# Columns picked by hand in a graph kernel: register loads moved to a fixed place in each unit, and an earlier request for the destination indices

## The chip, the cores and the metric

The kernel runs on one core of one Trainium2 chip. The metric is device time in microseconds of one execution. Nine executions of the kernel before were timed: median 5463.57 us, from 5436.52 to 5480.25 us.

## The reference: what is computed

One layer of a graph network over 12,500 nodes of 128 features and 400,000 edges, which come sorted by destination `dst`. With `h = relu(layernorm(x))`:

```
m   = relu(concat(h[src], h[dst], ea) @ w1 + b1) @ w2 + b2      # per edge; ea has 32 features
agg = segment_sum(m, dst)                                       # per node
gi  = agg @ w_ih + b_ih ;  gh = h @ w_hh + b_hh                 # a GRU cell
r, z = sigmoid(i_r + h_r), sigmoid(i_z + h_z) ;  n = tanh(i_n + r * h_n)
out = x + (1 - z) * n + z * h
```

Everything is float32.

## The kernel before, in words

**Stages.** A first stage (about the first 350 us) normalises the nodes, keeps `h` transposed in on-chip memory (`hT_all`, 128 features by 12,500 nodes) and writes the table `A = h @ w1[0:128]` to device memory. After it the edges are walked in 391 *pairs* (the change's words call them double groups) of 8 tiles of 128 edges; a pair is two *units* `u = 2k` and `u = 2k + 1` of 4 tiles each. Python loops write the instructions of all 782 units out one after another; each engine has one list of instructions in that order and runs it in order. No scheduler moves anything.

**One pair `k`.** POOL fetches the 1,024 rows `A[src]` with 8 indirect DMAs (line 146) into a buffer `G`; seven such buffers go round, and the next pair's fetch starts when the relu of the second unit of an older pair has let its buffer go. `Ld` holds the destinations of the edges, copied to 64 partitions; DVE compares them with node numbers to a one-hot matrix in the upper half of `L` (`onehot_T`, line 495); the lower half of `L` holds the edge features, which SP loads directly (line 485). `window` copies 2 x 32 columns of `hT_all` (`hw`, line 514), PE multiplies them by `w1[128:256]` (`oh`, line 517), and `window_rows` adds the bias into `RW` in two DVE instructions (line 526). PE then multiplies `L` by `RW` (`pre`, line 592), DVE adds the fetched rows (`add`, line 617), ACT applies the relu into `RB` (line 623), and PE sums the edges per node with a second one-hot matrix `OH` (DVE line 544; PE line 636, `seg`). `take` copies the sums out (DVE line 644, ACT line 645). Every 14 pairs a block of 512 nodes goes through the GRU in small steps (`node`).

**Pairs by hand.** 43 of the 391 pairs are not fetched by POOL. For 19 of them ACT, and for 18 DVE, collects the 1,024 columns `hT_all[:, src]` one instruction a column (lines 788 and 790); PE then multiplies them by `w1[0:128]` (line 603), and DVE's add of line 617 falls away. For the other 6 SP fetches the rows with one small DMA each (line 795). The address of a column is a register. An instruction of the engine itself, TENSOR_LOAD (line 782), loads 32 of these registers at a time, so a job of 1,024 columns has 32 such loads. A job is spread evenly over the units between the last pair of its kind and its own (36 to 46 units): `run_jobs` is called four times in a unit (phases 0 to 3), each time does as many groups of 4 columns as are due, and a load falls wherever 32 columns have been used up.

**Order within unit `u`:** phase 0 of the jobs; `take` (even units); `stages`: `onehot_T` (even) or `onehot` (odd) three pairs ahead, `pre(u + 3)`, `add(u + 2)`, `relu(u + 2)`; phase 1 of the jobs and `window` (even); phase 2; `seg(u)`; phase 3, `window_rows` (even) and a step of `node`.

**SP's list.** At every fourth unit `fetch(q + 2)` asks for `L` (256 KB) and then for `Ld` (two DMAs of 128 KB) of two pairs; both tiles have three buffers. Between them stand the row fetches of SP's own jobs.

Of the kernel before, what the change touches and what calls it, by code (L numbers as in the profile page):

```python
# [8 lines left out]
F32 = mybir.dt.float32  # L9
# [12 lines left out]
GRP = 4  # L22
# [5 lines left out]
V = 32  # L28
# [14 lines left out]
PLACE = 20  # L43
CH = PLACE * PAIR
LOAD = 32
STEP = {"act": 4, "dve": 4, "sp": 2}
SPREAD = {"act": 19, "dve": 18, "sp": 6}
NR = 12672

H_AT = 16512  # L50
# [6 lines left out]
def tile_gnn(ctx: ExitStack, tc: tile.TileContext, x, src, srcT, dstT, dstP, eaT, eaP, w1, b1, w2T, b2,  # L57
# [26 lines left out]

    mode, order = {}, {m: [] for m in SPREAD}
    for m, n in SPREAD.items():
        lo = JOBS0 + 15
        for i in range(n):
            k = lo + int((i + 0.5) * (NP - 2 - lo) / n)
            while k in mode:  # L90
                k += 1
            mode[k] = m
            order[m].append(k)
# [385 lines left out]
    def fetch(q):  # L479
        if q * QP >= NP:  # L480
            return
        n = min(QP, NP - q * QP)
        Ls[q] = p3.tile([128, QP * 512], F32, name="L")
        c = slice(q * QP * 512, (q * QP + n) * 512)
        nc.sync.dma_start(Ls[q][2 * V:, :n * 512], eaP[:, c])
        Ds[q] = p3.tile([2 * V, QP * 512], I32, name="Ld")
        for a in range(2):
            nc.sync.dma_start(Ds[q][V * a:V * (a + 1), :n * 512],
                              dstP[a:a + 1, c].to_broadcast([V, n * 512]))

    def onehot_T(k):
        if k >= NP:
            return
        c = slice((k % QP) * 512, (k % QP + 1) * 512)
        nc.vector.tensor_scalar(Ls[k // QP][:2 * V, c], Ds[k // QP][:, c], node_of[:, k:k + 1],  # L495
                                None, op0=ALU.is_equal)


    bases, PB_ = {}, {}

    def window(k):
        if k >= NP:
            return
        b = k // BP
        if k % BP == 0:
            n = min(BP, NP - k)
            _, vals = nc.values_load_multi_w_load_instructions(
                base_i[0:1, b, 0:n], engines=[ET.DVE], min_val=0, max_val=LAST,
                skip_runtime_bounds_check_because="clamped above")
            for i, v in enumerate(vals):  # L510
                bases[k + i] = v
        hw = p3.tile([128, 2, V], F32, name="hw", bufs=2)
        s = hT_all[:, bass.ds(bases.pop(k), V + SHIFT)]
        nc.vector.tensor_copy(hw, bass.AP(tensor=s.tensor, offset=s.offset,  # L514
                                          ap=[list(s.ap[0]), [SHIFT, 2], [1, V]]))
        PB_[k] = ps2.tile([128, 512], F32, name="oh")
        nc.tensor.matmul(PB_[k][:2 * V, :D], hw.rearrange("p a v -> p (a v)"), w1b,  # L517
                         start=True, stop=True)

    def window_rows(k):  # L520
        if k >= NP:
            return
        pm = PB_.pop(k)
        for a in range(2):
            s = slice(V * a, V * (a + 1))
            nc.vector.tensor_tensor(RW[k % 4][s, a, :], pm[s, :D], b1b[s, :], op=ALU.add)  # L526
# [80 lines left out]
    def add(u):  # L607
        if u >= NU:
            return
        if u in HE or u // 2 in hand:  # L610
            RT[u] = PP.pop(u)
            HE.pop(u, None)
            if u % 2:
                hand.pop(u // 2, None)
        else:
            RT[u] = unit(u)
            nc.vector.tensor_tensor(RT[u], PP.pop(u), RT[u], op=ALU.add)  # L617

    def relu(u):
        if u >= NU:  # L620
            return
        o = RB[u % 3]
        nc.scalar.activation(o[:, :, :D], RT.pop(u), AF.Relu)  # L623
        if u % 2:
            G.pop(u // 2, None)
# [142 lines left out]
        nc.sync.dma_start(at[r:r + 1, :], src[t0 * 128:(t0 + PAIR) * 128].rearrange(  # L768
            "(o e) -> o e", o=1))

    def one_by_one(m, k):
        et = {"act": ET.Activation, "dve": ET.DVE, "sp": ET.SP}[m]
        r = by_hand.index(k)
        if m == "sp":
            G[k] = pj[0].tile([128, GRP, 2, D], F32, name="G_sp", bufs=1)
            rows = G[k].bitcast(U8)
        else:
            hand[k] = pj[0].tile([128, PAIR * 128], F32, name=f"HE_{m}")
            he = hand[k].bitcast(U8)
        for e0 in range(0, PAIR * 128, LOAD):  # L780
            low, high = (0, ROW * (N - 1)) if m == "sp" else (H_AT, H_AT + 4 * (N - 1))
            _, vals = nc.values_load_multi_w_load_instructions(
                at[r:r + 1, e0:e0 + LOAD], engines=[et], min_val=low, max_val=high,
                skip_runtime_bounds_check_because="src holds numbers of nodes")
            for i, v in enumerate(vals):
                e = e0 + i
                if m == "act":
                    nc.scalar.copy(he[:, e * 4:e * 4 + 4], h_bytes[:, bass.ds(v - H_AT, 4)])  # L788
                elif m == "dve":
                    nc.vector.tensor_reduce(he[:, e * 4:e * 4 + 4],  # L790
                                            h_bytes[:, bass.ds(v - H_AT, 4), None],
                                            AX.X, ALU.max)
                else:
                    a, j = divmod(e // 128, GRP)
                    nc.sync.dma_start(rows[e % 128:e % 128 + 1, j, a, :],
                                      A_bytes[bass.ds(v, ROW)].rearrange("(o f) -> o f", o=1))
                if i % STEP[m] == STEP[m] - 1:
                    yield


    jobs = {}
    for m, kl in order.items():
        start = 2 * JOBS0
        for k in kl:
            end = 2 * k - (8 if m == "sp" else 4)
            jobs.setdefault(start, []).append((m, k, end - start))
            start = end if m != "sp" else 2 * k + 2
    live = {}

    PH = 4  # L810

    def run_jobs(u, phase):
        if u == 2 * JOBS0 and phase == 0:
            early.close()
            pj.append(late.enter_context(tc.tile_pool(name="pj", bufs=2, side="right")))
        if phase == 0:
            for m, k, span in jobs.get(u, ()):
                live[m] = [one_by_one(m, k), u, span, PAIR * 128 // STEP[m], 0]
        for m, job in list(live.items()):
            it, start, span, steps, done = job  # L820
            want = -(-steps * ((u - start) * PH + phase + 1) // (span * PH))
            while job[4] < want:
                job[4] += 1
                if next(it, "end") == "end":
                    del live[m]
                    break


    asked = [RAW]
# [9 lines left out]

    gathers(0)  # L840
    for q in range(2):
        fetch(q)
    for k in range(3):
        window(k)
        window_rows(k)


    def stages(u):
        if u + 7 >= 0:
            raw_stats(u + 7)  # L850
        if u + 6 >= 0:
            raw_fin(u + 6)
            raw_h(u + 6)
        if u % 2 == 0:
            onehot_T(u // 2 + 3)
        elif u > -7:
            onehot(u // 2 + 3)
        if u + 4 >= 0:
            raw_turn(u + 4)
        if u + 3 >= 0:  # L860
            pre(u + 3)
        if u + 2 >= 0:
            add(u + 2)
            relu(u + 2)

    for u in range(-7, 0):
        stages(u)
# [12 lines left out]
    for u in range(NU):  # L880
        k, h = divmod(u, 2)
        gathers(u)
        if h == 0:
            if k % QP == 0:
                fetch(k // QP + 2)
            if k % BP == 0 and k:
                nodes_left.append([node(k // BP - 1), 0])
            if k % PLACE == 1:
                indices(k // PLACE + 2)
            if k % PLACE == 5:  # L890
                place(k // PLACE + 1)
                dst_tile(k // PLACE + 2)
            if k == NP - 20:
                check_windows()
        for r in range(2 * u, min(2 * u + 2, NJ)):
            job_indices(r)
        if u == 2 * JOBS0 - 2:
            nc.vector.tensor_scalar(at, at, place_of[:, 0:1], place_of[:, 1:2],
                                    op0=ALU.mult, op1=ALU.add)

        def other(phase):
            run_jobs(u, phase)
            if h == 0 and phase == 1:
                window(k + 3)
            if h == 0 and phase == 3:
                window_rows(k + 3)
            if phase == 3:
                step(nodes_left)

        other(0)  # L910
        if h == 0:
            take(k - 1)
        stages(u)
        other(1)
        other(2)
        seg(u)
        if u == 0:
            node_setup()
        other(3)
# [173 lines left out]
```

## Time and profile before

| | |
|---|---|
| profiled execution, its own time | 5460.47 us |
| its span in the profile | 5458.6 us |
| median of nine executions | 5463.57 us |
| busy: PE, DVE, ACT, POOL | 3100.5, 2706.0, 2737.3, 2658.9 us |
| granted TensorE clock, mean | 0.657 |
| DMA traffic | 325.92 MB, 60 GB/s |

No engine is busy for more than 57% of the span. The forty slices look alike from about 350 us to the end, so one pair in the middle stands for the rest. In the groups of the profile the first number behind the bar is busy time, then the mean of one instruction, then the idle time of that engine in front of the group's instructions and what ended it; "issue" means that the profile shows nothing that the engine waited for. Instructions of an engine's sequencer, such as TENSOR_LOAD, are not counted as busy.

### The profile page before, as it was taken

How to read it: one execution, taken by the hardware profiler on the slowest of the kernel's cores; microseconds unless marked ns; L12 is line 12 of the kernel's file. 1: busy time of each engine (PE TensorE's matmuls, PEld its weight loads, DVE VectorE, ACT ScalarE, POOL GpSimd, SP SyncE). 2: the span in 40 equal slices, each digit the busy share in tenths (PEclk: the TensorE clock that was granted, in tenths of full speed). 3: DMA queues.
4: the chain of work that ended last, by engine and by line, in shares of the span. 5: the costliest groups of instructions: out<-in, count | busy, mean ns of one | idle time of the engine just before them, and what ended most of it. 6: DMA issues, size and time to landing. Idle time of an engine off the chain costs nothing. (4 is left out here: it accounts for less than half of the span.)

```text
span 5458.6 us, 94893 instructions
## 1 busy us (share of the span) xinstructions
PE 3100.5 (57%) x13578; PEld 1856.0 (34%) x13578; DVE 2706.0 (50%) x22515; ACT 2737.3 (50%) x20936; POOL 2658.9 (49%) x2789
## 2 busy tenths in 40 slices
PE   2663454555665656566555556555564656465657
PEld 2442232333333333333333333333332333233434
DVE  3644344545544544555555445554554554544553
ACT  2434344555555555555555555555555555555651
POOL 5345434354545454545554554455454454545562
PEclk7776666666665666566666666666665666666667
DMA  3322111222222122222222222222222221222221
GB/s 110 83 59 56 50 47 52 60 57 61 61 56 60 55 62 56 58 60 58 60 58 59 58 61 58 57 62 60 58 59 60 60 62 55 62 55 60 62 65 37
DMA packets 157887, 325.92 MB, mean 60 GB/s; under 512 B 65058, under 2 KB 77133, under 8 KB 157256
## 3 DMA queue, kind: packets, MB, share of 16 engines
q0 software_dynamic: 88992, 182.43, 12.0%
q1 hardware_dynamic: 68119, 137.33, 9.1%
q14 instruction: 520, 4.25, 0.3%
q8 instruction: 112, 1.84, 0.1%
q10 hardware_dynamic: 144, 0.07, 0.0%
HBM read 305.74 MB, written 13.84 MB: 59 GB/s over the span
## 5 line engine op out<-in xcount | busy, mean ns | idle before, releaser
L146 POOL DMA_INDIRECT G<-A,src_i x2704 | 2585.0, 956 | 2718.7 <-ACT RB L623 1823.5
L788 ACT COPY HE_act<-hT_all 128x4 uint8 x19456 | 2173.5, 191 | 1757.1 <-issue 1740.3
L790 DVE TENSOR_REDUCE HE_dve<-hT_all 128x4 uint8 x18432 | 1404.3, 144 | 1133.4 <-issue 1123.3
L592 PE MATMUL pre<-RW,L 128*128 128x256 f32 x3128 | 1355.7, 572 | 849.8 <-DVE G L617 703.9
L592 PEld LDWEIGHTS pre<-RW,L 128*128 128x128 f32 x3128 | 791.4, 280 | 1223.3 <-issue 707.7
L517 PE MATMUL oh<-w1b,hw 128*64 128x128 f32 x782 | 245.0, 411 | 1342.6 <-DVE hw L514 683.6
L636 PE MATMUL seg<-RB,OH 128*32 128x129 f32 x6250 | 719.6, 372 | 2.5 <-issue 2.5
L623 ACT ACTIVATE RB<-G 128x512 f32<-128x512 f32 x676 | 426.2, 630 | 469.8 <-issue 212.4
L517 PEld LDWEIGHTS oh<-w1b,hw 128*64 128x64 f32 x782 | 103.5, 188 | 1548.5 <-DVE hw L514 778.8
L526 DVE TENSOR_TENSOR RW<-oh,b1b 32x128 f32<-32x128 f32 x782 | 218.1, 279 | 770.0 <-issue 641.4
L617 DVE TENSOR_TENSOR G<-pre,G 128x512 f32<-128x512 f32 x676 | 460.5, 681 | 262.8 <-issue 243.8
L636 PEld LDWEIGHTS seg<-RB,OH 128*32 128x32 f32 x6250 | 384.4, 142 | 281.7 <-issue 183.0
L495 DVE TENSOR_SCALAR L<-Ld,node_of 64x512 f32<-64x512 int32 x391 | 189.6, 485 | 138.5 <-DMA Ld<-in_dstP 90.2
L644 DVE COPY sums<-seg 64x128 f32<-64x128 f32 x391 | 106.5, 272 | 187.2 <-remote 106.3
L645 ACT CAST dcol<-seg 64x1 f16<-64x1 f32 x391 | 60.0, 153 | 225.1 <-DVE sums L644 159.9
L544 DVE TENSOR_TENSOR OH<-dloc,iota 128x256 f32<-128x256 f16 (+1 forms) x392 | 162.1, 414 | 13.6 <-issue 10.8
L667 PEld LDWEIGHTS nd<-spot,sums 64*128 64x128 f32 x782 | 164.1, 320 | 13.3 <-issue 13.3
L667 PE MATMUL nd<-spot,sums 64*128 64x40 f32 x782 | 168.2, 404 | 0.0
L631 PE MATMUL seg<-zrow 1*64 1x129 bf16 x391 | 115.0, 294 | 0.0
L326 PE MATMUL pre<-w1a,hT_all 128*128 128x128 f32 x196 | 51.5, 412 | 77.2 <-issue 57.6
L686 PE MATMUL nd<-DEG,brow 33*128 33x512 f32 x112 | 94.0, 932 | 1.0 <-DVE DEG L654 1.0
L690 PE MATMUL nd<-TOT,w2ih 128*128 128x512 f32 x112 | 89.1, 890 | 0.0
(151 smaller groups left out, 1629.3 us busy)
## 6 DMA issues: line engine op xcount, KB each, us to landing
G_sp<-A SPq DMA_DIRECT2D x6144, 0.5 KB
L<-in_eaP SPq DMA_DIRECT2D x195, 256.0 KB
Ld<-in_dstP SPq DMA_DIRECT2D x390, 128.0 KB
G<-A,src_i POOLq DMA_INDIRECT x2704
xb<-in_x SPq DMA_DIRECT2D x28, 256.0 KB
out<-xb SPq DMA_DIRECT2D x28, 256.0 KB
xs<-in_x SPq DMA_DIRECT2D x11, 512.0 KB
A<-asb SPq DMA_DIRECT2D x11, 512.0 KB
```

Of the source, the lines that this page charges most:

```text
L146: nc.gpsimd.indirect_dma_start(out=G[k][:, j, a, :], out_offset=None, in_=table, in_offset=bass.IndirectOffsetOnAxis(ap=src_i[c][:, i:i + ...
L495: nc.vector.tensor_scalar(Ls[k // QP][:2 * V, c], Ds[k // QP][:, c], node_of[:, k:k + 1], None, op0=ALU.is_equal)
L517: nc.tensor.matmul(PB_[k][:2 * V, :D], hw.rearrange("p a v -> p (a v)"), w1b, start=True, stop=True)
L526: nc.vector.tensor_tensor(RW[k % 4][s, a, :], pm[s, :D], b1b[s, :], op=ALU.add)
L544: nc.vector.tensor_tensor(o, d.to_broadcast(shape), i.to_broadcast(shape), op=ALU.is_equal)
L592: nc.tensor.matmul(PP[u][:, 2 * i:2 * i + 2, :], Ls[k // QP][:, c0:c0 + 128], RW[k % 4], start=True, stop=not raw)
L617: nc.vector.tensor_tensor(RT[u], PP.pop(u), RT[u], op=ALU.add)
L623: nc.scalar.activation(o[:, :, :D], RT.pop(u), AF.Relu)
L636: nc.tensor.matmul(SEG[k][V * a:V * (a + 1), :D + 1], OH[k][:, j, a, :], RB[u % 3][:, (j % 2) * 2 + a, :D + 1], start=False, stop=all(b != ...
L667: nc.tensor.matmul(pt[:, bass.ds(offs[i], V + SHIFT)], sums[:, i, :], spot, start=False, stop=i == n - 1)
L788: nc.scalar.copy(he[:, e * 4:e * 4 + 4], h_bytes[:, bass.ds(v - H_AT, 4)])
L790: nc.vector.tensor_reduce(he[:, e * 4:e * 4 + 4], h_bytes[:, bass.ds(v - H_AT, 4), None], AX.X, ALU.max)
```

## The change

Four things are changed together.

1. **Destinations earlier.** `fetch` is split. `fetch_d` asks for `Ld`, and it is called for `q + 3`, ahead of `fetch(q + 2)`, which asks for `L` alone.
2. **First jobs.** Other pairs are chosen for the hand work (the same numbers: 18, 19 and 6), so that the first job of each kind is about as long as the others. DVE's jobs have 39 or 40 units, ACT's 36 to 40.
3. **Loads once a unit.** While DVE or ACT has a job, it loads 32 registers once in every unit. The load stands right behind a fixed place: DVE's add of line 617 (ACT: the relu of line 623) and the last 7 columns of the load before. The other 25 columns are spread over the four phases: 7 in phase 1, 6 in each of phases 2, 3 and 0. A job is therefore done in 32 units, and in the 4 to 8 units that are left before the next job starts the engine has no columns. SP's job keeps the even spread.
4. **Window.** `hw` is copied before the add of the even unit instead of in phase 1; its matmul stays in phase 1 (`window_b`).

```
-SPREAD = {"act": 19, "dve": 18, "sp": 6}
+TAIL = 7
+SPREAD = {"dve": 18, "act": 19, "sp": 6}
...
-        lo = JOBS0 + 15
+        lo, hi = {"dve": (JOBS0 + 3, NP - 14), "act": (JOBS0 + 11, NP - 6),
+                  "sp": (JOBS0 + 5, NP - 10)}[m]
         for i in range(n):
-            k = lo + int((i + 0.5) * (NP - 2 - lo) / n)
+            k = lo + int((i + 1) * (hi - lo) / n)
...
+    def fetch_d(q):
...
+        HW[k] = hw
+
+    def window_b(k):
...
+    class Job:
...
+        def run(self, left=0):
+            while len(self.vals) > left:
...
+    def behind(m, u):
+        if m in live:
+            live[m].run()
+            if live[m].e == PAIR * 128:
+                del live[m]
+        begin(m, u + 1)
+        if m in live:
+            j = live[m]
+            if j.loaded < PAIR * 128:
+                j.load(LOAD)
+            assert j.span * LOAD >= PAIR * 128
+
+    PARTS = (1, 2, 3, 0)
+
     def run_jobs(u, phase):
...
+        for m in ("act", "dve"):
+            if m in live:
+                n = max(0, len(live[m].vals) - TAIL)
+                live[m].run(TAIL + n - -(-n // (4 - PARTS.index(phase))))
...
         if u % 2 == 0:
             onehot_T(u // 2 + 3)
+            if u >= 0:
+                window(u // 2 + 3)
...
             add(u + 2)
+            behind("dve", u)
             relu(u + 2)
+            behind("act", u)
...
             if k % QP == 0:
+                fetch_d(k // QP + 3)
                 fetch(k // QP + 2)
...
             if h == 0 and phase == 1:
-                window(k + 3)
+                window_b(k + 3)
```

More of the change, by code (lines that the diff above doesn't have):

```diff
@@ L45 @@
 LOAD = 32
-STEP = {"act": 4, "dve": 4, "sp": 2}
-SPREAD = {"act": 19, "dve": 18, "sp": 6}
+TAIL = 7
+SPREAD = {"dve": 18, "act": 19, "sp": 6}
 NR = 12672
@@ L482, in fetch @@
         n = min(QP, NP - q * QP)
+        c = slice(q * QP * 512, (q * QP + n) * 512)
         Ls[q] = p3.tile([128, QP * 512], F32, name="L")
+        nc.sync.dma_start(Ls[q][2 * V:, :n * 512], eaP[:, c])
+    def fetch_d(q):
+        if q * QP >= NP:
+            return
+        n = min(QP, NP - q * QP)
         c = slice(q * QP * 512, (q * QP + n) * 512)
-        nc.sync.dma_start(Ls[q][2 * V:, :n * 512], eaP[:, c])
         Ds[q] = p3.tile([2 * V, QP * 512], I32, name="Ld")
@@ L496, in onehot_T @@
                                 None, op0=ALU.is_equal)
-    bases, PB_ = {}, {}
+    bases, PB_, HW = {}, {}, {}
     def window(k):
@@ L515, in window @@
                                           ap=[list(s.ap[0]), [SHIFT, 2], [1, V]]))
+        HW[k] = hw
+    def window_b(k):
+        if k >= NP:
+            return
         PB_[k] = ps2.tile([128, 512], F32, name="oh")
-        nc.tensor.matmul(PB_[k][:2 * V, :D], hw.rearrange("p a v -> p (a v)"), w1b,
+        nc.tensor.matmul(PB_[k][:2 * V, :D], HW.pop(k).rearrange("p a v -> p (a v)"), w1b,
                          start=True, stop=True)
@@ L769, in job_indices, with __init__, load @@
             "(o e) -> o e", o=1))
[L771 to L780, printed above, removed]
+    class Job:
+        def __init__(self, m, k, start, span):
+            self.m, self.k, self.start, self.span = m, k, start, span
+            self.e, self.loaded, self.vals = 0, 0, []
+            self.r = by_hand.index(k)
+            if m == "sp":
+                G[k] = pj[0].tile([128, GRP, 2, D], F32, name="G_sp", bufs=1)
+                self.to = G[k].bitcast(U8)
+            else:
+                hand[k] = pj[0].tile([128, PAIR * 128], F32, name=f"HE_{m}")
+                self.to = hand[k].bitcast(U8)
+        def load(self, n):
+            m = self.m
             low, high = (0, ROW * (N - 1)) if m == "sp" else (H_AT, H_AT + 4 * (N - 1))
+            et = {"act": ET.Activation, "dve": ET.DVE, "sp": ET.SP}[m]
             _, vals = nc.values_load_multi_w_load_instructions(
-                at[r:r + 1, e0:e0 + LOAD], engines=[et], min_val=low, max_val=high,
+                at[self.r:self.r + 1, self.loaded:self.loaded + n], engines=[et],
+                min_val=low, max_val=high,
                 skip_runtime_bounds_check_because="src holds numbers of nodes")
-            for i, v in enumerate(vals):
-                e = e0 + i
+            self.vals = list(vals)
+            self.loaded += n
+        def run(self, left=0):
+            while len(self.vals) > left:
+                v, e, m, to = self.vals.pop(0), self.e, self.m, self.to
+                self.e += 1
                 if m == "act":
-                    nc.scalar.copy(he[:, e * 4:e * 4 + 4], h_bytes[:, bass.ds(v - H_AT, 4)])
+                    nc.scalar.copy(to[:, e * 4:e * 4 + 4], h_bytes[:, bass.ds(v - H_AT, 4)])
                 elif m == "dve":
-                    nc.vector.tensor_reduce(he[:, e * 4:e * 4 + 4],
+                    nc.vector.tensor_reduce(to[:, e * 4:e * 4 + 4],
                                             h_bytes[:, bass.ds(v - H_AT, 4), None],
@@ L794, in one_by_one, with begin @@
                     a, j = divmod(e // 128, GRP)
-                    nc.sync.dma_start(rows[e % 128:e % 128 + 1, j, a, :],
+                    nc.sync.dma_start(to[e % 128:e % 128 + 1, j, a, :],
                                       A_bytes[bass.ds(v, ROW)].rearrange("(o f) -> o f", o=1))
-                if i % STEP[m] == STEP[m] - 1:
-                    yield
-    jobs = {}
+    starts = {}
     for m, kl in order.items():
-        start = 2 * JOBS0
+        start = 2 * JOBS0 + (m != "sp") + (16 if m == "act" else 0)
         for k in kl:
             end = 2 * k - (8 if m == "sp" else 4)
-            jobs.setdefault(start, []).append((m, k, end - start))
+            starts[m, start] = (k, end - start)
             start = end if m != "sp" else 2 * k + 2
     live = {}
-    PH = 4
+    def begin(m, u):
+        if (m, u) in starts:
+            live[m] = Job(m, starts[m, u][0], u, starts[m, u][1])
+    def behind(m, u):
[10 more added lines that the diff above has]
+    PARTS = (1, 2, 3, 0)
     def run_jobs(u, phase):
@@ L815, in run_jobs @@
             pj.append(late.enter_context(tc.tile_pool(name="pj", bufs=2, side="right")))
+        for m in ("act", "dve"):
+            if m in live:
+                n = max(0, len(live[m].vals) - TAIL)
+                live[m].run(TAIL + n - -(-n // (4 - PARTS.index(phase))))
         if phase == 0:
[L817 to L826, printed above, removed]
+            begin("sp", u)
+        if "sp" in live:
+            j = live["sp"]
+            want = -(-PAIR * 128 * ((u - j.start) * 4 + phase + 1) // (j.span * 4))
+            while j.e < want:
+                if not j.vals:
+                    j.load(LOAD)
+                j.run(max(0, len(j.vals) - (want - j.e)))
+            if j.e == PAIR * 128:
+                del live["sp"]
     asked = [RAW]
@@ L841, in tile_gnn @@
     for q in range(2):
+        fetch_d(q)
         fetch(q)
+    fetch_d(2)
     for k in range(3):
         window(k)
+        window_b(k)
         window_rows(k)
```

## The prediction

> **What bounds the kernel now.** I read the head of the page, then the costly groups, then one pair instruction by instruction, and last I counted over all records between 600 and 5,200 us (665 units). The chain that ended last has eight pieces, all after 5,451 us, so it says nothing of the middle.
>
> ```profile
> span 5458.6 us, 94893 instructions
> ...
> PE 3100.5 (57%) x13578; PEld 1856.0 (34%) x13578; DVE 2706.0 (50%) x22515; ACT 2737.3 (50%) x20936; POOL 2658.9 (49%) x2789
> ```
> ```profile
> L146 POOL DMA_INDIRECT G<-A,src_i x2704 | 2585.0, 956 | 2718.7 <-ACT RB L623 1823.5
> L788 ACT COPY HE_act<-hT_all 128x4 uint8 x19456 | 2173.5, 191 | 1757.1 <-issue 1740.3
> L790 DVE TENSOR_REDUCE HE_dve<-hT_all 128x4 uint8 x18432 | 1404.3, 144 | 1133.4 <-issue 1123.3
> L526 DVE TENSOR_TENSOR RW<-oh,b1b 32x128 f32<-32x128 f32 x782 | 218.1, 279 | 770.0 <-issue 641.4
> L495 DVE TENSOR_SCALAR L<-Ld,node_of 64x512 f32<-64x512 int32 x391 | 189.6, 485 | 138.5 <-DMA Ld<-in_dstP 90.2
> ```
>
> POOL waits 1,823 us for the relu that frees its buffers, so POOL is not the bound; DVE and ACT stand idle for "issue" in front of columns and, on DVE, between the two `RW` adds. Part of that is register loads, listed by line:
>
> ```profile
> L782 ACTq TENSOR_LOAD <-at x608: 1964/1992/2504, 354.3 to 5307.0; - x152
> L782 DVEq TENSOR_LOAD <-at x576: 2096/2116/2652, 366.8 to 5316.3; - x192
> ```
>
> A load takes about 2 us; meanwhile the engine works off what is queued. The other part shows in DVE's timeline (start, length, what, count, idle before). POOL's eight fetches of this pair start from 1610.38 to 1619.11, 1.25 us apart; the next run starts at 1624.87.
>
> ```profile
> 1614.01 0.20 DVE L790 TENSOR_REDUCE HE_dve<-hT_all 128x4 uint8 x2
> 1614.66 0.22 DVE L790 TENSOR_REDUCE HE_dve<-hT_all 128x4 uint8 x2 [0.44 <-issue]
> 1616.08 0.22 DVE L790 TENSOR_REDUCE HE_dve<-hT_all 128x4 uint8 x2 [1.21 <-issue]
> 1616.81 0.16 DVE L790 TENSOR_REDUCE HE_dve<-hT_all 128x4 uint8 x1 [0.51 <-issue]
> ...
> 1620.36 0.16 DVE L790 TENSOR_REDUCE HE_dve<-hT_all 128x4 uint8 x1 [0.55 <-issue]
> 1621.06 0.28 DVE L526 TENSOR_TENSOR RW<-oh,b1b 32x128 f32<-32x128 f32 x1 [0.55 <-issue]
> 1621.86 0.28 DVE L526 TENSOR_TENSOR RW<-oh,b1b 32x128 f32<-32x128 f32 x1 [0.52 <-issue]
> 1622.16 0.60 DVE L790 TENSOR_REDUCE HE_dve<-hT_all 128x4 uint8 x8
> 1622.68 0.41 DVE L544 TENSOR_TENSOR OH<-dloc,iota 128x256 f32<-128x256 f16 x1
> 1623.12 0.69 DVE L617 TENSOR_TENSOR G<-pre,G 128x512 f32<-128x512 f32 x1
> ```
>
> Columns normally start 0.064 us apart; from 4.3 us into the run they start on a grid of 0.71 us, ACT's on the same grid. At 11.4 us, 1.65 us after the last fetch ended, all runs fast again. I call these 11.4 us the run's **shadow**. The same holds for almost every run of 8 fetches. After the shadow DVE does the rest of its list up to the odd unit's add (the **tail**); the relu follows, and 1.06 us (median) after that add the next run starts. My count of DVE's time in the 293 stretches from one run to the next (us):
>
> ```
>                                          total   busy  idle in loads  other idle
> first 4.5 us of the shadow               1318.5   926       258          134
> rest of the shadow                       2051     485       216         1350
> tail, no pair by hand between             358     336         8           14
> tail with a pair by hand (39 of them)     481     335        92           54
> from the odd add to the next run          376     253       121            3
> ```
>
> So the sum of the path is shadow + tail + 1.06 us: 254 stretches without a pair by hand take 14.08 us, the 39 with one 25.9 us. Of DVE's idle time in loads only 100 us lie in tails.
>
> **The change part by part**, against the profiled execution's own 5460.47 us (span 5458.6 and 1.87 around it), which is 3.1 us below the median.
>
> *Destinations earlier.* `Ld(q+2)` stood behind `L` on SP and was asked 2 units before its first use counted in the list; now it has 4 units, some 28 us, more. The longest wait for it is 16.5 us, so they all end. The idle time in front of line 495 is 90.2 us for `Ld` and 41.1 us with SP's row fetches named, the same wait: 131 us, the upper bound; the lower is 0, as a wait inside the shadow costs nothing. A straight-line fit of the run-to-run times to what was in them gives 0.21 us a us of wait (standard error 0.04): 28 us; the pairs by hand add some. I take **-35**. SP's new wait, for line 495 of an earlier pair, ends before the wait of `L` behind it (for PE's `pre`, 643 us in all at line 485), so `L`, the row fetches and the node loads queued behind lose nothing. `L` is asked 1 us later and used 3 units after `Ld`: covered.
>
> *Loads behind long operations.* Between 600 and 5,200 us a load costs DVE 0.92 us of idle (median 1.03) and ACT 0.86. Behind the new place lie the add (0.681) and 7 columns (7 x 0.064): 1.13 us, against 2.116 + 0.088 to the first new column. If nothing else is queued, the gap is 1.07 us, worse than now. At a load's start up to 10 instructions were still waiting (10 is the commonest count on ACT, 239 of 570; on DVE 123 of 613). With 10, `L` (0.485) and `hw`, or `OH` (0.414), wait too: a gap of 0.5 to 0.66. I take 0.55. What this is worth: the tails with a pair by hand hold two loads, 39 x 2 x 0.55 = 43 instead of 92, -49; the other tails at most -8; at the shadow's start 0.88 us a stretch become about 0.6, four more columns done before the grid, worth up to 0.28 x 213 stretches with a tail = 60, at least 0: I take 25. Together **-80** (0 to -258). On ACT the relu (0.630) and 7 x 0.096 cover 1.30 of 2.06 us, a gap of 0.76; ACT waits for DVE in the tails (129 of 358 us idle), so 0 of it counts.
>
> [...]
>
> *Crowding.* The number of columns stays, but a pair now has 64 on an engine or none, where stretches without a pair by hand had 52.9 (DVE) and 56.1 (ACT). The fit gives 0.077 us an ACT column: an ACT-free pair would fall to 9.8 us, but its shadow alone is 11.4, so 1.6 us x 254 x 6/38 are lost: **+65**. On DVE, stretches with 64 columns took 14.87 us against 14.41 of all in the fit: +0.46 x 80% x 254 = +93. A stretch without any is not in the trace; the ends are 11.4 (shadow) and 14.4. I take 11.9, by the run at 1836 us, where the odd add ended inside the shadow and the next run came 11.8 us after: -2.5 x 20% x 254 = -127. DVE together **-34**.
>
> *Rest.* `hw` ahead of the even add delays it by 0.1 us (391 x 0.1 = +39 at most), and its matmul is done before `RW` asks (waits of `RW` for PE: 78 us in three rows): both lie in the shadow, **0**. PE and SP get 180 and 194 more sequencer waits of 17 ns, beside idle time: 0. First jobs: 0.
>
> Sum: -35 - 80 + 65 - 34 = -84: 5,376, or **5,380 us** beside the median.
>
> **The rivals.** *Slower, by the grid.* In a crowded pair DVE's list from odd add to 4.5 us into the run (5.56 us) holds 39 columns (2.5), the block of `sums`, `L`, `hw`, add (1.4) and two gaps (1.1): 0.6 us remain, 9 of the next 19 columns. The other 10 fall on the grid, where the pair shown did 8 in 4.3 us; then it fits. If the grid starts at 4.3 us, or ACT's 8 extra columns bring it on earlier, 7 to 16 columns and the first `RW` come after the shadow: +0.73 to +1.3 us. It decides from 0.73 us x 203 crowded stretches = 148, which equals the gains (115, and 98 if free pairs take the 12.47 us of the nine runs without row fetches) less the 65. At +1.2: 244 + 65 - 115 - 98 = +96: 5,560 us, up to 5,620. For it: before, only some 6 columns and `RW` were left for the grid. Against: in the fit a DVE column costs 0.018 us (0.005). [...]
>
> *Much faster.* If early loads and waits count in full (258 less 0.3 x 293 = -170, the tails -57, `Ld` -131, the two of crowding as above, +31): -327, 5,130 us; with half of it 5,290.
>
> *No change.* Shadow and tail keep their length whatever is done in the shadow: only hand tails and a little `Ld`, against the floor of ACT-free pairs: 5,447 to 5,480.
>
> **How the numbers follow.** Forecast (5,290 to 5,447) 0.46, slower by the grid (5,480 to 5,620) 0.34, much faster 0.11, no change 0.09. About 0.3% (16 us) is what a measurement of this kernel can tell from no change. Faster 0.57, same 0.09, slower 0.34. The range leaves out the far ends of both outer cases, about 0.1 each: 5,200 to 5,600; the forecast's own is above.
>
> **What the profile after would show.** The idle time of line 495 for `Ld` near 0; the same 576 and 608 loads; less "issue" in front of line 790; stretches between runs in two groups, near 14.8 and near 12 us. Wrong I am if more than 7 columns stand behind the shadow in crowded pairs, if DVE's gap at a load is 1 us or more, or if pairs without columns still take 14 us.

## The result and the profile after

The changed kernel takes 5,516.28 us (median of 10 runs, 5,506.99 to 5,531.17) where the kernel before takes 5,456.45 (31 runs): a ratio of 1.011, 95% interval 1.0092 to 1.0129. It is 60 us slower; the forecast was 5,380. The profiled execution has a span of 5,521.7 us.

The first view is the page of the changed kernel, the lines that answer to those shown of before (a line number is that of the new file: 816 was 790, 814 was 788, 539 was 526, 503 was 495).

```profile
span 5521.7 us, 95284 instructions
...
PE 3079.7 (56%) x13578; PEld 1843.3 (33%) x13578; DVE 2761.4 (50%) x22515; ACT 2699.1 (49%) x20936; POOL 2663.5 (48%) x2789
...
L148 POOL DMA_INDIRECT G<-A,src_i x2704 | 2589.7, 958 | 2774.2 <-ACT RB L636 1878.7
L814 ACT COPY HE_act<-hT_all 128x4 uint8 x19456 | 2133.3, 189 | 1508.1 <-issue 1490.0
L816 DVE TENSOR_REDUCE HE_dve<-hT_all 128x4 uint8 x18432 | 1438.5, 145 | 1476.8 <-issue 1468.2
...
L636 ACT ACTIVATE RB<-G 128x512 f32<-128x512 f32 x676 | 424.7, 629 | 677.1 <-DVE G L630 381.3
...
L539 DVE TENSOR_TENSOR RW<-oh,b1b 32x128 f32<-32x128 f32 x782 | 217.2, 278 | 389.3 <-issue 251.2
...
L503 DVE TENSOR_SCALAR L<-Ld,node_of 64x512 f32<-64x512 int32 x391 | 185.3, 474 | 2.7 <-issue 2.4
```

`L` no longer waits (138.5 before, 2.7 now). DVE's idle time in front of columns has grown from 1,133 to 1,477 us, and the relu waits 381 us for DVE's add, where it waited 92.7 before: the wait has moved. The relu's line of before:

```profile
L623 ACT ACTIVATE RB<-G 128x512 f32<-128x512 f32 x676 | 426.2, 630 | 469.8 <-issue 212.4 <-DVE G L617 92.7 <-ACT HE_act L788 38.5
```

The loads themselves are the same in number and length:

```profile
L801 ACTq TENSOR_LOAD <-at x608: 1966/1988/2424, 469.9 to 5430.4; - x152
L801 DVEq TENSOR_LOAD <-at x576: 2096/2116/2673, 357.1 to 5312.8; - x192
```

The second view is DVE's timeline of one pair with 64 columns on both engines. POOL's eight fetches start from 2946.28 to 2955.09, so the shadow ends near 2957.7; the next run starts at 2961.42.

```profile
2949.64 0.68 DVE L630 TENSOR_TENSOR G<-pre,G 128x512 f32<-128x512 f32 x1
2950.24 0.52 DVE L816 TENSOR_REDUCE HE_dve<-hT_all 128x4 uint8 x7
2951.30 0.16 DVE L816 TENSOR_REDUCE HE_dve<-hT_all 128x4 uint8 x1 [0.54 <-issue]
2952.02 0.22 DVE L816 TENSOR_REDUCE HE_dve<-hT_all 128x4 uint8 x2 [0.56 <-issue]
...
2956.98 0.16 DVE L816 TENSOR_REDUCE HE_dve<-hT_all 128x4 uint8 x1 [0.54 <-issue]
2957.68 0.66 DVE L816 TENSOR_REDUCE HE_dve<-hT_all 128x4 uint8 x9 [0.54 <-issue]
2958.26 0.56 DVE L539 TENSOR_TENSOR RW<-oh,b1b 32x128 f32<-32x128 f32 x2
2958.84 0.47 DVE L816 TENSOR_REDUCE HE_dve<-hT_all 128x4 uint8 x6
2959.23 0.41 DVE L557 TENSOR_TENSOR OH<-dloc,iota 128x256 f32<-128x256 f16 x1
2959.67 0.69 DVE L630 TENSOR_TENSOR G<-pre,G 128x512 f32<-128x512 f32 x1
```

In the pair shown of before, eight columns were left when the shadow ended at 1621.8, and the second `RW` add started just then. Here 15 columns and both `RW` adds are left, and the odd add ends 2.7 us after the shadow. ACT's timeline of the same pair shows that it is little better off: 22 copies are left when the shadow ends. They end at 2959.85; ACT then stands idle for 0.67 us, and the odd relu starts at 2960.52, 0.16 us after the add's end at 2960.36. So the add came last here, with ACT's list close behind it in length.

```profile
2956.27 0.29 ACT L814 COPY HE_act<-hT_all 128x4 uint8 x2 [0.51 <-issue]
2957.66 2.19 ACT L814 COPY HE_act<-hT_all 128x4 uint8 x22 [1.11 <-issue]
2960.52 0.63 ACT L636 ACTIVATE RB<-G 128x512 f32<-128x512 f32 x1 [0.67 <-ACT HE_act L814]
```

My counts over the stretches from one run of eight fetches to the next, without a pair by hand between, 600 to 5,200 us (those under 19 us; 60 columns or more are counted as 64). "Behind" means after the shadow's end and ahead of the odd add, for ACT ahead of the odd relu; "relu" is its start, us after the shadow's end. "Add last" counts the stretches in which the relu starts within 0.2 us of the end of its own unit's add, so that DVE's list was the last to end:

```
                                 stretches  us    DVE behind  RW behind  ACT behind  relu   add last
before, all                         254   14.08      4.0        0.6         9.1     1.69     161
changed, all                        242   14.68      6.8        1.0        15.9     2.29     151
changed, 64 on both                 139   14.96     10.1        1.5        18.9     2.59     114
changed, no DVE column               29   14.26      0          0.1        16.7     1.88       0
changed, at most 3 ACT columns       31   14.35      6.7        1.0         0       2.01      30
```

(242 x 0.60 = 145 us; the stretches with 64 on both alone give 139 x 0.88 = 122. Left out are runs that follow each other with no pause of POOL: seven groups in the changed kernel, of which the five without a pair by hand, 13 runs of eight, took 14.1 us a run.)

In the 114 crowded stretches where the add comes last, ACT had stood idle for 0.66 us in front of the relu (mean). That is about what a stretch without DVE columns gains on a crowded one, 0.70 us; there ACT's list is the last to end in all 29, and the add had been done 10 us earlier (mean).

Per pair, from the start of one pair's odd relu to the next one's, for pairs 62 to 379, and the time at which pair 62 begins, with the kernels of the experiments on chips of the same kind:

```
                                          pair 62 at   fetched pairs (280, 281)   pairs by hand (37, 38)
before                                       1061            13.52                    13.00
Ld ahead                                     1038            13.51                    12.98
Ld ahead, new pairs                           978            13.69                    12.89
Ld ahead, new pairs, crowded                 1026            14.14                    14.25
changed                                       996            14.00                    13.44
changed, even, aligned loads                  980            13.64                    12.31
changed, without DVE's columns                950            13.00                    13.14
```

So the changed kernel is 65 us ahead at pair 62 and loses that and 85 us more by pair 379 (4,280 us before for these pairs, 4,430 now); behind them it makes up some 20.

### The profile page after: what moved, and what is told of

Read it like the earlier page. It is cut to its first block, busy times and chain, and to the rows that moved or that the text cites. A ratio compares the mean times of both kernels' runs of the same rounds, so it can differ in the third digit from the quotient of the medians.

```text
span 5521.7 us, 95284 instructions
## 1 busy us (share of the span) xinstructions
PE 3079.7 (56%) x13578; PEld 1843.3 (33%) x13578; DVE 2761.4 (50%) x22515; ACT 2699.1 (49%) x20936; POOL 2663.5 (48%) x2789
## 3 DMA queue, kind: packets, MB, share of 16 engines
q0 software_dynamic: 88992, 182.43, 11.9%
## 5 line engine op out<-in xcount | busy, mean ns | idle before, releaser
L814 ACT COPY HE_act<-hT_all 128x4 uint8 x19456 | 2133.3, 189 | 1508.1 <-issue 1490.0
L816 DVE TENSOR_REDUCE HE_dve<-hT_all 128x4 uint8 x18432 | 1438.5, 145 | 1476.8 <-issue 1468.2
L649 PE MATMUL seg<-RB,OH 128*32 128x129 f32 x6250 | 701.5, 364 | 134.8 <-ACT RB L636 121.0
L699 PE MATMUL misc<-DEG,brow 33*128 33x512 f32 x112 | 72.0, 726 | 42.7 <-DVE gt L716 42.2
```

The costliest lines, as they stand in the source:

```text
L649: nc.tensor.matmul(SEG[k][V * a:V * (a + 1), :D + 1], OH[k][:, j, a, :], RB[u % 3][:, (j % 2) * 2 + a, :D + 1], start=False, stop=all(b != ...
L814: nc.scalar.copy(to[:, e * 4:e * 4 + 4], h_bytes[:, bass.ds(v - H_AT, 4)])
L816: nc.vector.tensor_reduce(to[:, e * 4:e * 4 + 4], h_bytes[:, bass.ds(v - H_AT, 4), None], AX.X, ALU.max)
```

## The experiments

The theory, formed from these counts: the loss is the *crowding*. 64 columns a pair leave columns and `RW` behind the shadow on both engines, and pairs with none on one engine gain little, since the other engine's list bounds them. The rivals: the place of the loads, or the new choice of pairs; and, for the pairs without columns, instructions that are held in the shadow, columns or none.

One thing must be told before the numbers. The runs fell on five chips. On two of them the kernel before takes 5,444 to 5,458 us, as in the first measurement, and shows the grid. On the other three it takes 3,713 to 3,715 us, and the kernels profiled there show no grid. Ratios are always to the kernel before on the same chip, and the two kinds are kept apart.

**Ld ahead alone.** The kernel before with `fetch_d`:

```
     for q in range(2):
+        fetch_d(q)
         fetch(q)
+    fetch_d(2)
...
+                fetch_d(k // QP + 3)
                 fetch(k // QP + 2)
```

> The kernel before with one edit: the destinations Ld are asked for 3 double groups ahead. My prediction's step says 35 us less than before (0 to 131): about 5,420. If the 77 us that the changed kernel gained up to unit 120 came from this part, about 5,380 and the gain stands early; if they came from the longer first jobs, 5,420 or more and the gain is spread over the whole span. In either case the idle time in front of L for Ld falls from 90 us to under 10.

Measured on a chip with the grid: 5,434.8 us, ratio 0.9962 (0.9943 to 0.998), 21 us less (11 to 31). The wait in front of `L` is gone:

```profile
L501 DVE TENSOR_SCALAR L<-Ld,node_of 64x512 f32<-64x512 int32 x391 | 190.4, 487 | 0.4 <-issue 0.4
```

Of 139 us of wait, 21 lay on the path, near the 28 of the prediction's fit. All of it is there by pair 62 (23 us ahead); afterwards the two kernels keep step to within 5 us.

**The new pairs too.** The same with the changed choice of pairs and starts, columns still spread evenly:

> The kernel before with Ld 3 ahead and with the changed kernel's pairs by hand (first jobs as long as the others), but columns spread evenly over a job and loads wherever a job's next 32 columns begin, as before. Theory (the loss of units 120 to 760 comes from having 64 columns a pair or none): this kernel has no such loss and keeps the gain at the start, 5,340 to 5,390. Rival (the new pairs or the shorter spans lose it): 5,480 to 5,530, near the changed kernel.

Measured: 5,405.4 us, 0.9919 (0.9891 to 0.9947), some 23 us less than with `Ld` alone (0.9919/0.9962). That is less than expected; the rival falls. At pair 62 it is 60 us further ahead, and it loses 48 of these by pair 379, where fetched pairs take 13.69 us instead of 13.51. Which of the first jobs brings the early gain (SP's first job, 122 units long instead of 82, or those of DVE and ACT) was not taken apart.

**Crowding at the old place of the loads.**

```
-                live[m] = [one_by_one(m, k), u, span, PAIR * 128 // STEP[m], 0]
+                live[m] = [one_by_one(m, k), u, span if m == "sp" else PAIR * 128 // LOAD,
+                           PAIR * 128 // STEP[m], 0]
```

> As the kernel with Ld 3 ahead and the new pairs, but each job of DVE and ACT does 32 columns a unit from its start and then pauses, as in the changed kernel; loads stay where the next 32 columns begin, not behind the add and the relu. Theory (crowding alone): 100 to 150 us more than the kernel with even columns, 5,470 to 5,530; DVE stretches with 64 columns take about 14.9 us. Rival (the place of the loads does it): as the kernel with even columns, 5,340 to 5,390.

Measured: 5,613.5 us, 1.0279 (1.0262 to 1.0296): 208 us more than the even spread, above the expected 100 to 150. Something else is in it: with exactly 32 columns a unit the load falls into phase 0 of every unit, in odd units right ahead of `OH` and the odd add. Counted over the loads of columns alone, DVE's gap from its last instruction ahead of a load to the first behind it is 1.73 us here, 1.32 with the even spread, 1.26 before and 0.91 in the changed kernel. So this run does not tell what crowding loses by itself from what the bad place of its loads loses.

**The even spread with the new place of the loads**, first try:

```
-                j.load(LOAD)
+                j.load(min(-(-PAIR * 128 // j.span), PAIR * 128 - j.loaded))
```

> The changed kernel with one edit: a job loads as many registers a unit as spread it evenly over its units (27 or 28 instead of 32), at the same place behind the add and the relu, with 7 columns kept back as before. Theory (crowding): the loss goes, 5,300 to 5,390, and stretches between runs of fetches return to 14.1 us or less. Rival (the place of the loads, or hw ahead of the even add): stays at 5,490 to 5,540.

Measured: 5,994.4 us, 1.0976. Neither theory had this. The groups of loads in this kernel (minimum, median, longest, in ns) show why:

```profile
L801 ACTq TENSOR_LOAD <-at x719: 1022/5833/6585, 490.8 to 5926.9; - x180
L801 DVEq TENSOR_LOAD <-at x718: 2066/2384/6723, 358.3 to 5804.9; - x180
```

On DVE a load of 27 registers took 2.38, 6.29, 6.32, 6.29 us in turn, one of 26 2.08 and 5.87 by turns; one of 28 on ACT took 1.73 (medians). The numbers are 4 bytes each, so the quick ones are just those that start at a multiple of 16 bytes. Loads of 32 always do. The run tells nothing of crowding.

**The even spread with aligned loads** (28 registers, or 32 in a job of 36 units):

```
+                n = -(-PAIR * 128 // j.span)
+                j.load(min(n + -n % 4, PAIR * 128 - j.loaded))
```

> As the kernel with 27 or 28 registers a unit, but every load takes a multiple of 4 (28, or 32 in a job of 36 units), so that each starts at a multiple of 16 bytes. In the run with 26 to 28 registers, loads from other starts took 5.8 to 6.3 us and those from a multiple of 16 bytes 1.7 to 2.4. Theory (start address): every load takes 1.9 us or less, and the crowding is gone with the loads still behind the add and the relu: the 5,405 of the kernel with Ld 3 ahead and new pairs less the 97 us by which the changed kernel beats the crowded one, 5,280 to 5,340. Rival (more loads a job are the loss, or even columns make the loads' place worthless): 5,400 or more.

This run fell on a chip without the grid: 3,578.7 us, 0.9628 (0.9608 to 0.9648). It says nothing of crowding on a grid, but it does show the loads: the median is 1.77 us on ACT and 1.86 on DVE, and none is over 2.6. POOL is the bound there; of its 2,703 pauses between fetches all but one are about 0.30 us:

```profile
L148 POOL DMA_INDIRECT G<-A,src_i x2704 | 2604.9, 963 | 836.4 <-issue 782.8
```

Once more, beside the changed kernel:

> The changed kernel, unchanged, once more. The chip of the last four runs gave 3,713 us for the kernel before, and its DVE and ACT show no grid behind POOL's fetches; the first runs' chip gave 5,457 us. If this call's chip is one like the first: 1.009 to 1.013 of before. If it is one like the last, theory (the loss was columns left on the grid): no loss there, 0.96 to 0.98 of before, since crowded columns then cost only DVE's and ACT's own time, which lies beside POOL's. Rival (the loss lies in the order of the lists, grid or none): slower than before there too, 1.01.

> The changed kernel with 28 registers a unit (32 in a job of 36 units), every load from a multiple of 16 bytes, once more beside the changed kernel. On a chip with the grid: 5,280 to 5,340 by the theory of crowding and start address (0.968 to 0.979 of before); 5,400 or more by its rival. On a chip without the grid: 0.963 of before as in the last runs, and within 1% of the changed kernel, as crowding then costs nothing.

Both ran on a chip with the grid. The changed kernel repeats its loss (5,514.9 us, 1.0135, 1.0075 to 1.0194); the even spread takes 5,380.4 us, 0.9894 (0.9835 to 0.9953). The one edit takes 135 us away, so the crowding is what the changed kernel pays for. The edit also makes each load shorter (28 registers instead of 32; medians 1.86 us instead of 2.12 on DVE), and DVE's gap at a load shrinks with it, from 0.91 to 0.61 us. The even spread with the old place of the loads speaks against this as the cause: its gap is 1.32 us, longer than either, and its fetched pairs take 13.69 us, not the changed kernel's 14.00. The hoped-for 5,280 to 5,340 is missed: against the even spread with the old place of the loads (0.9919, on another chip with the grid) the new place brings 0.25%, and the intervals overlap. From the old place to the new the gap went from 1.32 to 0.61 us, but the fetched pairs take 13.64 us against 13.69; only the pairs by hand gained plainly (12.31 against 12.89).

**Without columns.** Both engines' columns left out, and DVE's alone:

```
             live[m] = Job(m, starts[m, u][0], u, starts[m, u][1])
+            if m in ('act', 'dve'):
+                nc.vector.memset(live.pop(m).to.bitcast(F32), 0.0)
```

> The changed kernel without the columns and register loads of DVE and ACT (that work is left out; a memset fills each tile). Stretches between runs without columns on one engine took 14.2 to 14.3 us in the changed kernel. Theory (the other engine's 64 columns bound them): without either, 11.4 to 12.5 us a stretch, 4,450 to 4,700 in all. Rival (the instructions held in the shadow bound them, columns or none): about 14 us, 5,150 to 5,300.

> The changed kernel without DVE's and ACT's columns and their register loads (work left out, a memset fills the tiles), on a chip with the grid if this call has one. In the changed kernel, stretches without DVE columns took 14.09 us (29 of them, 64 ACT columns in each), those without ACT columns 14.43 (28). Theory (the engine that has 64 columns bounds a stretch, whichever it is): without either 11.4 to 12.5 us a stretch and 4,550 to 4,700 in all. Rival (instructions held in the shadow bound it, columns or none): about 14 us, 5,150 to 5,300. On a chip without the grid: 3,570 as before.

> The changed kernel without DVE's columns and loads only (work left out). Theory (ACT's list alone bounds a stretch at about 14 us): stretches with 64 ACT columns stay at 13.9 to 14.3 us and those with none of either fall to 11.4 to 12.5, 5,100 to 5,350 in all. My prediction's step (a pair free of DVE columns takes 11.9 us): about 4,700. On a chip without the grid: 3,560 to 3,590.

All three fell on chips without the grid: 3,570.3, 3,567.3 and 3,563.5 us. These say nothing of the grid. They do say that there evenly spread columns cost next to nothing: the kernel with all of them, with aligned loads, took 3,578.7. Again:

> The changed kernel without DVE's columns and loads (work left out), again. On a chip without the grid it took 3,563 us; on one with it, theory (ACT's 64 columns alone hold a stretch at about 14 us): stretches with 64 ACT columns stay at 13.9 to 14.3 us and those with none of either fall to 11.4 to 12.5, 5,100 to 5,350 in all. My prediction's step (a pair free of DVE columns takes 11.9 us): about 4,700.

On a chip with the grid: 5,181.8 us (one execution), inside the theory's 5,100 to 5,350 and far from the 4,700 of my prediction's step. The 209 stretches with 64 ACT columns took 13.88 us. What a pair without either engine's columns takes is not well shown: three such stretches (two of them with 3 ACT columns) took 11.6, 12.4 and 14.4 us, and 19 groups of runs that follow with no pause, 48 runs mostly where ACT has no columns, took 13.0 us a run, where 11.4 to 12.5 was expected. The views are DVE's and then ACT's timeline of one stretch (fetches from 3012.19 to 3021.14, next run at 3025.93):

```profile
3001.16 0.69 DVE L630 TENSOR_TENSOR G<-pre,G 128x512 f32<-128x512 f32 x1
...
3015.72 0.58 DVE L539 TENSOR_TENSOR RW<-oh,b1b 32x128 f32<-32x128 f32 x2 [1.23 <-issue]
3016.30 0.42 DVE L557 TENSOR_TENSOR OH<-dloc,iota 128x256 f32<-128x256 f16 x1
3016.76 0.69 DVE L630 TENSOR_TENSOR G<-pre,G 128x512 f32<-128x512 f32 x1
3026.84 0.28 DVE L657 COPY sums<-seg 64x128 f32<-64x128 f32 x1 [9.39 <-PE seg L649]
```

```profile
3017.21 0.19 ACT L814 COPY HE_act<-hT_all 128x4 uint8 x1 [0.43 <-issue]
...
3022.91 0.19 ACT L814 COPY HE_act<-hT_all 128x4 uint8 x1 [0.43 <-issue]
3023.61 1.52 ACT L814 COPY HE_act<-hT_all 128x4 uint8 x15 [0.51 <-issue]
3025.04 0.62 ACT L636 ACTIVATE RB<-G 128x512 f32<-128x512 f32 x1
```

Adds and relus counted in order, the relu at 3025.04 belongs to the add at 3001.16, which DVE had done 23 us before; the add at 3016.76 is already the next pair's. ACT's copies go at the grid's pace (starts about 0.71 us apart from 3017.21 to 3020.76), and 15 of them stand ahead of the relu when the shadow ends. Over the 209 stretches the add had ended 16.5 us before its relu (mean), and in 3 of them alone within 0.2 us. ACT alone holds the stretch at 13.9 us. (DVE's next instruction then waits for PE, whose `seg` needs the relu.)

**Where the columns stand in a pair.** One kernel issues columns only from behind the odd add to ahead of the even one, another spaces them out so that some stand between the `RW` adds and between `OH` and the odd add:

```
# columns early
+        l = [(v, p) for v in range(start, start + span) for p in range(PH)
+             if (p > 0 if v % 2 else p == 0)]
# columns between
         for a in range(2):
+            if a:
+                run_jobs(2 * (k - 3), 7)
...
+            if h and phase == 0:
+                onehot(k + 3)
```

> The kernel with Ld 3 ahead and new pairs, but DVE's and ACT's columns are issued only behind an odd unit's add and relu and up to the next even unit's (4 of 8 places of a pair), so that L, hw, the RW adds, OH and the odd add stand alone in the later part of the shadow. Theory (on the grid every start costs 0.71 us whatever its length, so long operations there and columns outside are better): 5,405 falls to 5,100 to 5,300. Rival (an instruction behind a two-operand one is held, to the end of the shadow if no column stands between): 5,400 to 5,650. If the place of the columns in a pair does not matter: 5,380 to 5,430.

> The kernel with Ld 3 ahead and new pairs, with columns in twice as many places of half the number, so that 2 to 4 columns stand between the two RW adds and between OH and the odd add. Theory (in the shadow the instruction behind a two-operand one is held, 2.9 us between the RW adds in 165 stretches before and 2.1 behind OH in 105): four to five more columns a stretch are done in the shadow, 0.1 to 0.3 us less a stretch, 5,330 to 5,390. Rival (the hold is only the grid): 5,395 to 5,415.

> Ld 3 ahead and new pairs, with DVE's and ACT's columns only from behind an odd unit's add to ahead of the even unit's. On a chip with the grid, theory (each start on the grid costs 0.71 us whatever its length): 0.94 to 0.98 of before. Rival (an instruction behind a two-operand one is held until the shadow's end if no column stands between): 1.0 to 1.04. On a chip without the grid 1.06, as in the earlier run.

> Ld 3 ahead and new pairs, with columns in twice as many places of half the number, so that 2 to 4 stand between the RW adds and between OH and the odd add. On a chip with the grid, theory (the instruction behind a two-operand one is held): 5,330 to 5,390, 0.977 to 0.988 of before. Rival (only the grid): as the kernel with Ld ahead and new pairs, 0.989 to 0.994. On a chip without the grid 0.983, as in the earlier run.

> Ld 3 ahead and new pairs, with DVE's and ACT's columns only from behind an odd unit's add to ahead of the even unit's, for a chip with the grid if this call has one. There, theory (each start on the grid costs 0.71 us whatever its length): 0.94 to 0.98 of before. Rival (the time of a stretch goes by how many instructions an engine's list holds, wherever they stand): 0.985 to 1.0. Second rival (the columns, all early, bring the grid on earlier, or an instruction behind a two-operand one is held to the shadow's end): 1.0 to 1.06. On a chip without the grid 1.06, as in two earlier runs.

> The changed kernel with 28 aligned registers a unit, and with columns in twice as many places, so that some stand between the two RW adds and between OH and the odd add. On a chip with the grid, theory (the instruction behind a two-operand one is held, so that columns between them are done for nothing): 0.978 to 0.986 of before, against the 0.989 of the kernel without the edit. Rival (only the grid): 0.987 to 0.992. On a chip without the grid, where POOL is the bound: 0.960 to 0.966.

All six ran on chips without the grid, so that their question stays open for chips with the grid. Columns early: 3,950.9, 3,950.5 and 3,947.8 us (1.0636, 1.0637, 1.062). Columns between: 3,650.2 and 3,649.8 us (0.9826, 0.9824). The spacing on top of the even aligned loads, the last kernel: 3,578.3 us, 0.9625 (0.9609 to 0.9641), the same as without it (0.9628). The early columns lose there because POOL waits again for the relu that frees its buffers:

```profile
L147 POOL DMA_INDIRECT G<-A,src_i x2704 | 2593.1, 959 | 1203.1 <-issue 785.7 <-ACT RB L630 384.8 <-DMA G<-A,src_i 16.8
```

**The changed kernel a third time**, meant for a chip without the grid:

> The changed kernel, unchanged, for a chip without the grid if this call has one. There, theory (the loss was columns left on the grid): 0.96 to 0.98 of before, close to the 0.963 of the even spread with aligned loads. Rival (the order of the lists loses, grid or none): 1.01. On a chip with the grid: 1.009 to 1.015.

It fell on one with it: 5,523.5 us, 1.0125 (1.0084 to 1.0166). What the changed kernel does on a chip without the grid was never measured.

**A version that beats both** on a chip of the kind that the case was measured on is the changed kernel with 28 aligned registers a unit: 0.9894 of before, against 1.0135 beside it. The kernel with `Ld` ahead and new pairs alone is nearly as good (0.9919).

## Why the prediction was wrong

*Destinations earlier* (-35, 0 to -131): right within its range. 21 us (11 to 31) measured alone, and `L`'s wait near 0.

*Loads behind long operations* (-80): oversized. Beside an even spread the new place is worth about 14 us (0.9894 against 0.9919 of 5,456, not told from 0). What failed is the worth of a gap. Counted as in the experiments, but over all loads, DVE's mean gap went from 1.20 us before to 0.85 after (median 1.24 to 1.07), ACT's from 0.93 to 0.78. My prediction had 0.92 and 0.86 before, by a count that came out lower, and 0.55 and 0.76 after. So DVE's gap did not reach 0.55, but it fell by 0.35 us, nearly the 0.37 forecast. From the even spread at the old place to the even aligned loads it fell further, from 1.25 to 0.58, and in the profiled executions that brought little: the fetched pairs gained 0.05 us (280 of them, 14 us) where 25 us was priced for the shadow's start, and the pairs by hand 0.58 us (38 of them, 22 us) where 49 us was priced for their tails.

I took 0.55 us because 10 waiting instructions were the commonest count on ACT and common on DVE. After the change 7 instructions started during a load in 245 of the 598 loads on DVE, and 10 in 180; the median gap of 1.07 us is what a load leaves when the add and 7 columns alone cover it, the prediction's figure for a load with nothing else queued. The 180 loads with 10 do not fit it.

Beside crowded columns the changed kernel is 97 us below the crowded one with the old place (5,516 against 5,613). Much of that may be that kernel's own bad place, ahead of the odd add; the number doesn't bear on the forecast's step, which started from an even spread.

*Crowding* (+65 on ACT, -34 on DVE): this decided the sign. Its cost is 118 to 135 us (1.011 less 0.9894, on 5,456 us; 135 in the runs side by side), not 31. The term of crowded pairs was about right in size for one pair: 14.87 us taken, 14.96 measured, for 139 stretches with 64 on both. The term that failed is that of the free pairs. I priced each engine as though the other's list were not there: 11.9 us for a pair without DVE columns, and a floor of 11.4 without ACT's. They take 14.26 and 14.35, because the other engine has its 64 columns in most of them; the run without any DVE column shows ACT holding a stretch at 13.9. Without the -127 the sum would have come out at +43, slower. A maximum of two lists was added up like a sum.

Which list is the longer one is seen from the relu and the add of its own unit. In crowded stretches it is DVE's (114 of 139), by about 0.7 us, so that taking DVE's columns away can gain no more than that before ACT's list holds the pair, as it does in all 29 stretches without them. There ACT's columns set the time, and the -127 left them out. In stretches with at most 3 ACT columns DVE's list holds (30 of 31). Why fewer DVE columns are then left behind the shadow, 6.7 instead of 10.1, is open.

*Rest and first jobs* (0): -23 us for the new pairs as a whole; in the profiled executions 60 us were gained early, 48 given back and some 15 gained behind pair 379. The `hw` copy ahead of the even add was not tried alone; it is part of every kernel with the new place of the loads.

The four measured steps, -21 - 23 - 14 + 118, are the +60, by the way they are made: the last is what is left. They come from ratios taken on two chips of the same kind, so the last digit of each means little.

*The rival.* "Slower, by the grid" is what happened, by its own marks: it spoke of 7 to 16 columns and the first `RW` behind the shadow in crowded pairs, and of 0.73 to 1.3 us; measured are 10.1 columns, 1.5 of the two `RW` adds, and 0.88 us. My test "more than 7 columns behind the shadow" is met by the mean and by 79 of the 139 crowded stretches, and so is "pairs without columns still take 14 us". What I held against it, the 0.018 us a column of the fit, came from stretches with 51 columns on average, where 4.0 were left; it says little of 64. Its time of 5,560 was too high because fewer stretches than the 203 were crowded on both engines (139 of 242). On a chip with the grid ACT keeps to it even with no tensor_reduce column left: in the run without DVE's columns 5.4% of ACT's starts between 600 and 5,200 us came 680 to 740 ns after the one before (5.4% in the kernel before), against 1.3% for the same kernel on a chip without the grid.

## What to carry to other kernels

When two engines each have a list to finish before the same hand-over, price a pair by the later list, not by adding what each would gain: work taken off one engine in a stretch is worth at most the time by which the other's list ends earlier, here about 0.7 us. Where, as on the chips with the grid, only part of the background work fits into cover, spread it evenly: the part that no longer fits costs (here 118 to 135 us), and the pairs that have none give little back. Take the starts of register loads at multiples of 16 bytes before any other comparison with another load size: here 27 registers on DVE took 2.38 us from there and 6.3 from elsewhere.

## What was not expected of the hardware

A register load costs by where it starts. From a multiple of 16 bytes 32 registers took 1.99 us on ACT and 2.12 on DVE, and 28 took 1.73 and 1.86; from elsewhere 26 to 29 took 5.6 to 6.3 (medians). An odd rest costs more than a whole four: 27 aligned registers took 2.38 us on DVE, more than 28 and more than 32.

The grid belongs to the chip, or to its condition. The same program took 5,444 to 5,458 us on two chips and 3,713 to 3,715 on three; on the latter columns ran 0.06 (DVE) and 0.1 us (ACT) apart beside POOL's fetches (medians), and in the even kernel with aligned loads POOL fetched with pauses of 0.30 us alone. What makes the difference was not found, and nothing in these traces tells of it. It also means that the verdict on this change holds for chips with the grid only, and that the questions put to the others (whether long operations or columns are cheaper on the grid) are open.

The grid is not the columns' own: PE shows it too. In the run without DVE's columns on a chip with the grid, POOL made 24 fetches from 2145.5 us on with pauses of 0.30 us alone, and eleven small matmuls of one step of `node` started at multiples of about 0.70 us from each other. In the whole run such matmuls start 0.03 us apart (median). Like the columns they take an address from a register; whether that matters was not tried.

```profile
2155.56 0.20 PE L685 MATMUL misc<-spot_h,dcol 128*128 128x40 f16 x1 [0.55 <-issue]
2157.65 0.19 PE L685 MATMUL misc<-spot_h,dcol 128*128 128x40 f16 x1 [1.89 <-issue]
2159.06 0.19 PE L685 MATMUL misc<-spot_h,dcol 128*128 128x40 f16 x1 [1.22 <-issue]
```

They took 22 us, and DVE stood idle for 27.6 us meanwhile. In the even kernel with aligned loads, on a chip without the grid, none of these matmuls starts more than 0.1 us after the one before it within a step. So in this place a pair without columns on either engine is not free of the grid: POOL runs on, and PE goes at the grid's pace.
